# Layer 1's attention: transposes by query tile and two pieces later, values and output products put off, cosine product in place

## The chip, the cores and the metric

The kernel runs on one core of one Trainium2 chip. The metric is the device time of one execution in microseconds (us), the median of several runs.

## The reference, cut to what matters

Four layers act on 4 sequences of 512 tokens of width 256, all in fp32. Each layer normalises its input and adds an attention branch and a feed-forward branch to it. The change touches the attention branch of layer 1 alone, a latent attention with 16 heads:

```
q   = rmsnorm(x @ wq_a) @ wq_b                  # per head: 128 columns without, 64 with rotation
ckv = x @ wkv_a                                 # 64 compressed columns, 64 rotated key columns
k_nope, v = split(rmsnorm(ckv[:64]) @ wkv_b)
q_pe = q_pe * cos + rotate_half(q_pe) * sin     # likewise k_pe
scores = (q_nope . k_nope + q_pe . k_pe) * 192 ** -0.5, causal
out = softmax(scores) @ v, all heads, @ wo
```

Beside it layer 1 has a product-key branch (each token picks 8 of 512 experts, whose rows are gathered from memory) and a gated MLP.

## The kernel before, in words

**Streams and pieces.** Each branch is a Python generator that emits instructions and yields at the end of each piece a number, its planned cost in us. `weave` takes the next piece from the stream that is least far along, relative to its planned total. In layer 1 three streams are woven: `latent_pieces` (the attention), `product_key_pieces` and `glu_pieces`. The program order that comes out is the priority in which a scheduler, with its own estimate of durations, fills each engine's instruction queue; an instruction that it takes to be ready may go ahead of earlier ones on its engine. `tc.keep_in_program_order` ties one instruction behind the one emitted just before it on the same engine. On the chip each engine works through its queue and waits at semaphores.

**Heads and pairs.** The head's key and value weights are folded into the query and the output weights (`carry`, once per group of four heads), so keys and values of all heads are the same latent rows: `kf` (keys, with the rotated part) and `cv` (values, 64 columns). A pair `p` is two heads of one sequence; there are 32 pairs, and `s` from 0 to 63 counts head by head. The loop has four pieces per `s`, `i` from 0 to 3, one for each tile of 128 query tokens.

- `queries(p)` (L707 on): the four query products (L715 to L718), ACT's copy `pes` of the part to be rotated (L721), four transfers on SP's queue that copy `pes` to `psw` with halves of 32 partitions swapped (L723), and the unrotated part into `qf` (L725, L726). It is emitted in piece 1 of the even head before the pair.
- `rotate` (L730 on), three pieces later, on DVE: `pec` = `pes` times cosine (L732), `psw` times sine in place (L733), and two additions into `qf` (L734, L735).
- `probabilities(s, i)`: through `exp_scores` one score product into a bank of the kind "mm" (L577), DVE's mask and minimum into `pr` (L580), ACT's exponential with row sum (L584). After `i` = 3 DVE takes the reciprocal of the sums (L747) and ACT scales the four `pr` tiles (L749).
- `turned(s - 1, j)`: transposes on TensorE of the previous head (L756). For key tile `j` it turns the blocks of query tiles `j` to 3 into one of two banks "tr"; the copy to `PT` (L760) is emitted one piece later, on DVE for even `j` (512 and 256 columns wide), on ACT for odd `j` (384 and 128). `PT` holds 1280 columns, one run for each key tile.
- After the last copy of a pair's second head: the value product, 16 matmuls into a bank "acc" (L800), ACT's copy to `zT` (L806), and after each second pair four output products into banks "acc" (L813), each followed by DVE's addition to `x` in `add_scaled` (L142). The four are emitted one after another, each a piece of its own.

Banks: four "mm", two "tr", two "acc"; the gated MLP's output products (L194) use "acc" as well. The SBUF pool has two buffers for each name unless `bufs` says otherwise.

Of the kernel before, what the change touches and what calls it, by code (L numbers as in the profile page):

```python
# [14 lines left out]
P = 128  # L15
NB, SEQ, DM = 4, 512, 256
# [586 lines left out]
def latent_pieces(c, a, keep, prep, open_pool):  # L603
# [102 lines left out]
    def queries(p):  # L706

        g, b, pair = p // 8, p // 2 % 4, p % 2
        if p % 8 == 0:
            carry(g)  # L710
        wpe0, wpe1, wl0, wl1, _ = weights[g]
        tokens = slice(b * SEQ, (b + 1) * SEQ)
        cols = slice(pair * P, (pair + 1) * P)
        pe, pl = c.ps(), c.ps()
        nc.tensor.matmul(pe, lhsT=wpe0[:, cols], rhs=qa0[:, tokens], start=True, stop=False)  # L715
        nc.tensor.matmul(pl, lhsT=wl0[:, cols], rhs=qa0[:, tokens], start=True, stop=False)
        nc.tensor.matmul(pe, lhsT=wpe1[:, cols], rhs=qa1[:KL, tokens], start=False, stop=True)
# [3 lines left out]
        nc.scalar.copy(pes, pe)  # L721
        for to in range(0, P, 32):
            nc.sync.dma_start(psw[to : to + 32, :], pes[to ^ 32 : (to ^ 32) + 32, :])  # L723
        qf = c.tile(pool, [P, 2, SEQ], "qf")
        nc.scalar.mul(qf[:KL, 0, :], pl[:KL, :], -scale)  # L725
        nc.scalar.mul(qf[KL:, 1, :], pl[KL:, :], -scale)  # L726
        qfs[p] = qf
        return pes, psw, qf

    def rotate(pes, psw, qf):  # L730
        pec = c.tile(pool, [P, SEQ], "pec", bufs=1)
        nc.vector.tensor_mul(pec, pes, cosq)  # L732
        tc.keep_in_program_order(nc.vector.tensor_mul(psw, psw, sinq))  # L733
        nc.vector.tensor_add(qf[:KL, 1, :], pec[:KL, :], psw[:KL, :])  # L734
        nc.vector.tensor_add(qf[KL:, 0, :], pec[KL:, :], psw[KL:, :])  # L735

    def probabilities(s, i):
        p, h = s // 2, s % 2
        b = p // 2 % 4
        if i == 0:  # L740
            totals[s] = c.tile(pool, [P, TPB], "total")
        rinv = totals[s]
        prs[s].append(exp_scores(
            c, pool, late, qfs[p][:, h, :], kf[:, h, b * SEQ : (b + 1) * SEQ], i, rinv[:, i : i + 1]
        ))
        if i == TPB - 1:
            nc.vector.reciprocal(rinv, rinv)  # L747
            for j, pr in enumerate(prs[s]):
                nc.scalar.mul(pr, pr, rinv[:, j : j + 1])  # L749

    def turned(s, j):

        pt = c.ps("tr")
        n = SEQ - j * P
        for i in range(j, TPB):
            nc.tensor.transpose(  # L756
                pt[:, (i - j) * P : (i - j + 1) * P], prs[s][i][:, j * P : (j + 1) * P], c.ident
            )
        copy = nc.scalar.copy if j % 2 else nc.vector.tensor_copy
        return lambda: copy(PTs[s][:, START[j] : START[j] + n], pt[:, :n])  # L760

    START = (0, 512, 896, 1152)
    qfs, prs, totals, PTs, zTs = {}, {}, {}, {}, {}
    rotate(*queries(0))
    copy = None
    yield 4.5
    for s in range(65):
        if s < 64:
            prs[s] = []
        for i in range(TPB):  # L770
# [8 lines left out]
            if i == 0 and s % 2 == 1 and s < 63:  # L779
                rotate(*turning)  # L780
            yield 0.85
            if i == 1 and s % 2 == 0 and s < 62:
                turning = queries(s // 2 + 1)
                yield 2.6
        if copy:
            copy()
            copy = None
        if s > 0:
            del prs[s - 1]
        if s % 2 == 1:  # L790
            continue
        if s == 0:
            continue
# [11 lines left out]
        zTs[pair] = c.tile(pool, [P, SEQ], "zT", bufs=3)  # L805
        nc.scalar.copy(zTs[pair], z)  # L806
        yield 2.1
        if pair == 1:
            wz = weights[g][4]
            for t in range(TPB):  # L810
                po = c.ps("acc")[:, :DM]
                for k in range(2):
                    nc.tensor.matmul(  # L813
                        po, lhsT=zTs[k][:, t * P : (t + 1) * P], rhs=wz[:, k, :],
                        start=(k == 0), stop=(k == 1),
                    )
                add_scaled(c, b * TPB + t, po)
                if g == 3 and t == TPB - 1:
                    c.part_done(b)
                yield 0.85  # L820


def product_key_pieces(c, a, keep, pool, dram, xn):
# [594 lines left out]
```

## Time and profile before

| | |
|---|---|
| median of 3 runs | 3323.99 us (3313.49 to 3325.25) |
| the profiled execution, its own time | 3325.63 us |
| its span | 3323.9 us, granted TensorE clock 0.99 |
| busy in the span: PE, DVE, ACT, POOL | 97%, 57%, 38%, 17% |
| first and last score product of layer 1 | 903.3 and 1572.9 us after the start |
| 900 to 1600 us, busy: PE, DVE, ACT, POOL | 667.97, 502.41, 421.68, 123.86 us |

PE is TensorE's matmuls, PEld its weight loads, DVE VectorE, ACT ScalarE, POOL GpSimd, SP the engine that only issues transfers. Names such as L756 are lines of the kernel before. The ends of matmuls are modelled in the profile, and so a PE that is busy in it is not one at its peak; the starts of matmuls are recorded. A wait is given to the engine and line whose signal came last. Waiting loads of weights cost nothing so long as the matmul before them still runs.

### The profile page before, as it was taken

The page shows a single profiled execution, that of the slowest core. Times are in us where ns is not written, and L with a number is a line of the kernel's source. Part 1 is how long each engine was busy: PE and PEld are TensorE (multiplying, and loading weights), DVE is VectorE, ACT ScalarE, POOL GpSimd, SP SyncE. Part 2 cuts the span into 40 slices and gives each one's busy share as a digit, 9 for nine tenths or more (in the row PEclk, how much of TensorE's full clock was granted, in tenths as well). Part 3 has the DMA queues.
Part 4 walks back from the last instruction along what each step waited for, and adds up shares of the span by engine and source line. Part 5 has one row for each costly group of instructions (what it writes and reads, how often), then busy time and mean ns, then how long its engine had stood idle before and what let it go on. Part 6 is the DMA issues. An engine that isn't in the chain of part 4 may idle for free.

```text
span 3323.9 us, 35406 instructions
## 1 busy us (share of the span) xinstructions
PE 3209.1 (97%) x12524; PEld 1921.4 (58%) x12524; DVE 1894.4 (57%) x4720; ACT 1255.3 (38%) x2870; POOL 579.8 (17%) x445
## 2 busy tenths in 40 slices
PE   8999999998899999999999999999999999999999
PEld 4556555655555555455655555556556665555555
DVE  4777778877788678656655545455455532222222
ACT  4444454443565645568322333333333311111111
POOL 0465556655212133100000000000000000000000
PEclk9999999998999999999999999999999999999999
DMA  3233323323213254301001000000000000000000
GB/s 124 77 105 96 125 85 105 102 96 115 59 43 98 50 146 127 90 14 42 15 1 53 5 1 26 0 20 7 0 20 1 1 19 19 20 21 20 17 0 26
DMA packets 75650, 165.14 MB, mean 50 GB/s; under 512 B 12368, under 2 KB 46288, under 8 KB 70608
## 3 DMA queue, kind: packets, MB, share of 16 engines
q1 hardware_dynamic: 64368, 127.20, 11.9%
q0 software_dynamic: 10240, 33.56, 4.1%
q8 instruction: 98, 1.61, 0.2%
q10 hardware_dynamic: 864, 2.12, 0.2%
q14 instruction: 80, 0.66, 0.1%
HBM read 149.08 MB, written 4.85 MB: 46 GB/s over the span
## 4 chain that ended last, share of the span: by engine, by line
PE 72%; DVE 12%; DMA 6%; issue 4%; POOL 4%; ACT 2%; SPq 0%; DVEq 0%; another core or an unknown queue 0%; POOLq 0%; ACTq 0%
PE mm L125 30%; PE acc L194 10%; PE mm L577 7%; PE mm L133 4%; PE acc L1027 4%; PE acc L593 3%; DMA G<-own 3%; DVE cy L259 2%; PE tr L1023 2%; DVE G L400 2%; DMA e<-in_p_experts,ids 2%; PE tr L756 1%; PE acc L813 1%; PE tr L486 1%; PE acc L800 1%
## 5 line engine op out<-in xcount | busy, mean ns | idle before, releaser
L125 PE MATMUL mm<-xnT,wu 128*128 128x512 f32 x2384 | 1083.4, 597 | 9.2 <-DVE cy L259 4.7
L125 PEld LDWEIGHTS mm<-xnT,wu 128*128 128x128 f32 x2384 | 444.8, 191 | 462.9 <-issue 426.4
L584 ACT ACTIVATE pr<-pr,nm 128x128 f32<-128x128 f32 (+3 forms) x512 | 286.6, 560 | 257.9 <-DVE nm L580 234.0
L186 ACT ACTIVATE sg<-mm 128x512 f32<-128x512 f32 x200 | 119.0, 595 | 697.7 <-PE mm L125 697.5
L187 DVE TENSOR_TENSOR hT<-sg,mm 128x512 f32<-128x512 f32 x200 | 136.9, 684 | 424.3 <-PE mm L125 415.3
L194 PE MATMUL acc<-wu,hT 128*128 128x256 f32 x1600 | 374.1, 382 | 0.0
L194 PEld LDWEIGHTS acc<-wu,hT 128*128 128x128 f32 x1600 | 300.7, 191 | 89.4 <-issue 34.8
L580 DVE CUSTOM_DVE_ANT_0 pr<-mm,late 128x128 f32<-128x128 f32 (+3 forms) x512 | 245.5, 486 | 70.4 <-PE mm L577 55.3
L125 PE MATMUL mm<-xnT,w_in 128*128 128x512 f32 x512 | 231.5, 596 | 6.6 <-DVE cy L259 5.1
L144 DVE SCALAR_TENSOR_TENSOR x<-acc,cw,x 128x256 f32<-128x256 f32 x256 | 123.3, 483 | 182.0 <-PE acc L194 177.1
L917 POOL DMA_INDIRECT e<-in_p_experts,ids x128 | 129.8, 1014 | 359.4 <-DVE x L144 315.1
L400 DVE TENSOR_TENSOR_SCAN G<-G,eye 128x1024 f32<-128x1024 f32 x64 | 155.6, 2431 | 56.4 <-DMA G<-own 56.3
L577 PE MATMUL mm<-kf,qf 128*128 128x128 f32 (+3 forms) x512 | 177.7, 448 | 7.8 <-DVE qf L735 4.4
L1024 DVE COPY PT<-tr 128x128 f32<-128x128 f32 (+3 forms) x256 | 118.7, 481 | 107.1 <-PE tr L1023 107.0
L426 POOL TENSOR_TENSOR G<-G,CB 128x1024 f32<-128x1024 f32 x64 | 151.1, 2361 | 142.2 <-ACT CB L352 81.3
L259 DVE SCALAR_TENSOR_TENSOR cy<-mm,ws,cy 128x509 f32<-128x509 f32 (+2 forms) x216 | 158.4, 741 | 28.9 <-ACT cy L255 25.6
L125 PEld LDWEIGHTS mm<-xnT,w_in 128*128 128x128 f32 x512 | 96.6, 191 | 111.0 <-issue 96.9
L412 ACT ACTIVATE xD<-xc,ws 128x128 f32<-128x128 f32 x256 | 84.3, 391 | 197.7 <-POOL y L449 191.7
L142 DVE TENSOR_TENSOR x<-acc,x 128x256 f32<-128x256 f32 x176 | 73.9, 421 | 148.1 <-PE acc L593 121.1
L577 PE MATMUL mm<-k,q 128*128 128x128 f32 (+3 forms) x512 | 154.9, 446 | 0.8 <-ACT k L1005 0.8
L1027 PE MATMUL acc<-PT,V 128*128 128x512 f32 (+3 forms) x512 | 148.8, 434 | 0.0
L1027 PEld LDWEIGHTS acc<-PT,V 128*128 128x128 f32 x512 | 97.4, 190 | 82.6 <-issue 32.7
(247 smaller groups left out, 4601.3 us busy)
## 6 DMA issues: line engine op xcount, KB each, us to landing
G<-own SPq DMA_DIRECT2D x64, 512.0 KB
w_in<-in_m_units SPq DMA_DIRECT2D x16, 1024.0 KB
eb<-since SPq DMA_DIRECT2D x96, 128.0 KB
wu<-in_o_units SPq DMA_DIRECT2D x8, 1536.0 KB
wo<-in_m_units SPq DMA_DIRECT2D x16, 512.0 KB
psw<-pes SPq DMA_DIRECT2D x128, 64.0 KB
wu<-in_g_units SPq DMA_DIRECT2D x4, 1536.0 KB
wu<-in_f_units SPq DMA_DIRECT2D x4, 1536.0 KB
```

What stands on the lines that cost most here:

```text
L125: c.nc.tensor.matmul(out, lhsT=w[:, d, cols], rhs=c.xnT[:, d, tokens], start=(d == 0), stop=(d == 1))
L133: c.nc.tensor.matmul(out, lhsT=c.xnT[:, d, tokens], rhs=w[:, d, cols], start=(d == 0), stop=(d == 1))
L187: nc.vector.tensor_mul(h, sg, pu)
L194: nc.tensor.matmul(po, lhsT=hT[k][:, t * P : (t + 1) * P], rhs=wd[:, k, :], start=(i == 0), stop=(i == per - 1),)
L259: nc.vector.scalar_tensor_tensor(y[:, j:], src[:, : SEQ - j], conv[:, k, 3 - j : 4 - j], y[:, j:], ALU.mult, ALU.add,)
L400: nc.vector.tensor_tensor_scan(flat, flat, eye.rearrange("p h t -> p (h t)"), 0.0, ALU.mult, ALU.add)
L426: nc.gpsimd.tensor_mul(G, G, seqs[b][2][:, t, :][:, None, :].to_broadcast([P, HG, P]))
L577: nc.tensor.matmul(sc, lhsT=q[:, i * P : n], rhs=k[:, :n], start=True, stop=True)
L580: nc.vector.tensor_tensor_reduce(out=pr, in0=sc, in1=late[:, SEQ - n :], scale=1.0, scalar=-NEG, op0=ALU.add, op1=ALU.min, accum_out=nm,)
L584: nc.scalar.activation(pr, pr, AF.Exp, bias=nm, scale=-1.0, accum_out=total)
L917: nc.gpsimd.indirect_dma_start(out=e, out_offset=None, in_=a["p_experts"], in_offset=bass.IndirectOffsetOnAxis(ap=ids[:, t, k : k + 1], ax ...
L1027: nc.tensor.matmul(z[:, j * P :], lhsT=V[:, j, h, :], rhs=PT[:, j, j * P :], start=(j == 0), stop=(j == TPB - 1),)
```

## The change

- `turned(s, i)` now goes by query tile `i`: it turns the `i` + 1 blocks of one `pr` tile, and one copy spreads them over `PT`, which is laid out so that the blocks of one key tile lie side by side (1664 columns). Copies of query tiles 1 and 3 (256 and 512 columns) are on DVE, of 0 and 2 (128 and 384) on ACT.
- It is emitted two pieces later: for head `s` in pieces 2 and 3 of the next head and 0 and 1 of the one after. The value product follows after piece 1 of the second head after the pair, two pieces later than before.
- The four output products are put in a list, and one is emitted at the end of each following piece.
- `rotate` writes the cosine product over `pes`; `pec` is gone. `wl0` and `wl1` have one buffer each.

```
-        wl0 = c.tile(pool, [P, 256], "wl0")
-        wl1 = c.tile(pool, [P, 256], "wl1")
+        wl0 = c.tile(pool, [P, 256], "wl0", bufs=1)
+        wl1 = c.tile(pool, [P, 256], "wl1", bufs=1)
...
     def rotate(pes, psw, qf):
-        pec = c.tile(pool, [P, SEQ], "pec", bufs=1)
-        nc.vector.tensor_mul(pec, pes, cosq)
+        nc.vector.tensor_mul(pes, pes, cosq)
         tc.keep_in_program_order(nc.vector.tensor_mul(psw, psw, sinq))
-        nc.vector.tensor_add(qf[:KL, 1, :], pec[:KL, :], psw[:KL, :])
-        nc.vector.tensor_add(qf[KL:, 0, :], pec[KL:, :], psw[KL:, :])
+        nc.vector.tensor_add(qf[:KL, 1, :], pes[:KL, :], psw[:KL, :])
+        nc.vector.tensor_add(qf[KL:, 0, :], pes[KL:, :], psw[KL:, :])
...
-    def turned(s, j):
-
+    def turned(s, i):
+
+        if i == 0:
+            PTs[s] = c.tile(pool, [P, LEAD * TPB + P], "PT")
+        PT, pr, n = PTs[s], prs[s][i], (i + 1) * P
+        prs[s][i] = None
         pt = c.ps("tr")
-        n = SEQ - j * P
-        for i in range(j, TPB):
-            nc.tensor.transpose(
-                pt[:, (i - j) * P : (i - j + 1) * P], prs[s][i][:, j * P : (j + 1) * P], c.ident
-            )
-        copy = nc.scalar.copy if j % 2 else nc.vector.tensor_copy
-        return lambda: copy(PTs[s][:, START[j] : START[j] + n], pt[:, :n])
-
-    START = (0, 512, 896, 1152)
+        for j in range(i + 1):
+            cols = slice(j * P, (j + 1) * P)
+            nc.tensor.transpose(pt[:, cols], pr[:, cols], c.ident)
+
+        out = v3(PT, P)[:, i : i + LEAD // P * i + 1 : LEAD // P, :]
+        copy = nc.vector.tensor_copy if i % 2 else nc.scalar.copy
+        return lambda: copy(out, v3(pt[:, :n], P))
+
+    LEAD = SEQ - P
...
+    waiting = []
     yield 4.5
-    for s in range(65):
+    for n in range(65 * TPB + 2):
+        s, i = n // TPB, n % TPB
         if s < 64:
-            prs[s] = []
-        for i in range(TPB):
-            if s < 64:
-                probabilities(s, i)
-            if s > 0:
-                if i == 0:
-                    PTs[s - 1] = c.tile(pool, [P, 1280], "PT")
-                ready, copy = copy, turned(s - 1, i)
-                if ready:
-                    ready()
...
+            if i == 0:
+                prs[s] = []
+            probabilities(s, i)
+        if n >= TPB + 2 and n - TPB - 2 < 64 * TPB:
+            ready, copy = copy, turned(*divmod(n - TPB - 2, TPB))
+            if ready:
+                ready()
+        elif copy:
+            copy()
+            copy = None
+        if i == 0 and s % 2 == 1 and s < 63:
+            rotate(*turning)
+        yield 0.85
+        if i == 1 and s % 2 == 0 and s < 62:
+            turning = queries(s // 2 + 1)
+            yield 2.6
+        if waiting:
+            yield waiting.pop(0)()
+        if not (i == 1 and s % 2 == 1 and s > 1):
+            continue
+
         if copy:
             copy()
             copy = None
...
-                    rhs=PTs[s - 2 + h][:, START[j] : START[j] + SEQ - j * P],
+                    rhs=PTs[2 * p + h][:, j * LEAD + j * P : j * LEAD + SEQ],
...
+        def output(t, g=g, b=b, wz=weights[g][4], zT=dict(zTs)):
+            po = c.ps("acc")[:, :DM]
+            for k in range(2):
+                nc.tensor.matmul(
+                    po, lhsT=zT[k][:, t * P : (t + 1) * P], rhs=wz[:, k, :],
+                    start=(k == 0), stop=(k == 1),
+                )
+            add_scaled(c, b * TPB + t, po)
+            if g == 3 and t == TPB - 1:
+                c.part_done(b)
+            return 0.85
+
         if pair == 1:
-            wz = weights[g][4]
-            for t in range(TPB):
-                po = c.ps("acc")[:, :DM]
...
-                yield 0.85
+            waiting = [lambda t=t, o=output: o(t) for t in range(TPB)]
+    for o in waiting:
+        yield o()
```

More of the change, by code (lines that the diff above doesn't have):

```diff
@@ L765, in latent_pieces @@
     copy = None
+    waiting = []
     yield 4.5
-    for s in range(65):
+    for n in range(65 * TPB + 2):
+        s, i = n // TPB, n % TPB
         if s < 64:
-            prs[s] = []
-        for i in range(TPB):
-            if s < 64:
-                probabilities(s, i)
-            if s > 0:
-                if i == 0:
-                    PTs[s - 1] = c.tile(pool, [P, 1280], "PT")
-                ready, copy = copy, turned(s - 1, i)
-                if ready:
-                    ready()
-            if i == 0 and s % 2 == 1 and s < 63:
-                rotate(*turning)
-            yield 0.85
-            if i == 1 and s % 2 == 0 and s < 62:
-                turning = queries(s // 2 + 1)
-                yield 2.6
+            if i == 0:
[18 more added lines that the diff above has]
+            continue
         if copy:
@@ L787, in latent_pieces @@
             copy = None
[L788 to L793, printed above, removed]
         p = s // 2 - 1
@@ L801, in latent_pieces @@
                     z[h * KL : (h + 1) * KL, j * P :], lhsT=cv[:, b * TPB + j, :],
-                    rhs=PTs[s - 2 + h][:, START[j] : START[j] + SEQ - j * P],
+                    rhs=PTs[2 * p + h][:, j * LEAD + j * P : j * LEAD + SEQ],
                     start=(j == 0), stop=(j == TPB - 1),
                 ))
-        zTs[pair] = c.tile(pool, [P, SEQ], "zT", bufs=3)
-        nc.scalar.copy(zTs[pair], z)
+        zT = zTs[pair] = c.tile(pool, [P, SEQ], "zT", bufs=3)
+        nc.scalar.copy(zT, z)
         yield 2.1
-        if pair == 1:
-            wz = weights[g][4]
-            for t in range(TPB):
-                po = c.ps("acc")[:, :DM]
[L812 to L820, printed above, removed]
+        def output(t, g=g, b=b, wz=weights[g][4], zT=dict(zTs)):
[9 more added lines that the diff above has]
+            return 0.85
+        if pair == 1:
+            waiting = [lambda t=t, o=output: o(t) for t in range(TPB)]
+    for o in waiting:
+        yield o()
 def product_key_pieces(c, a, keep, pool, dram, xn):
```

## The prediction

> **What bounds the kernel now.** I read the page's slices first (TensorE, PE, at nine tenths or more nearly everywhere), then the table of 50 us stretches over layer 1's attention (900 to 1600 us), then the waits of that window, then its timeline. Five stretches; the columns are PE, PEld, DVE, ACT, POOL busy us, granted clock, DMA share, GB/s:
>
> ```profile
> 1100.00:1150.00 50.00, 50.00 (x202) 26.82 (x202) 31.55 (x93) 33.24 (x89) 5.78 (x6) 1.00 0.15 41
> 1150.00:1200.00 50.00, 46.98 (x201) 26.20 (x197) 37.65 (x125) 28.09 (x73) 19.80 (x21) 1.00 0.61 149
> 1200.00:1250.00 50.00, 44.77 (x181) 25.42 (x181) 36.10 (x121) 23.55 (x64) 17.18 (x17) 0.93 0.61 144
> 1300.00:1350.00 50.00, 44.43 (x190) 26.44 (x189) 38.72 (x138) 27.13 (x74) 21.18 (x21) 0.97 0.52 131
> 1450.00:1500.00 50.00, 50.00 (x225) 30.40 (x224) 31.09 (x87) 30.67 (x79) 0.00 (x0) 1.00 0.05 11
> ```
>
> PE is the bound; DVE and ACT have a quarter to a half free. Where the expert gathers run (POOL near 20) PE still loses 3 to 6 us in 50. So only PE's stalls can be won. The waits (engine and line, what it waited for: us in total, times, longest):
>
> ```profile
> PEld tr L756 <- ACT pr L749: 40.3, 83, 1.4
> DVE prod L927 <- DMA e<-in_p_experts,ids: 41.8, 41, 3.8
> DVE pec L732 <- ACT pes L721: 18.5, 9, 5.0
> PEld acc L813 <- DVE x L142: 12.6, 8, 3.1
> PE acc L813 <- DVE x L142: 9.5, 7, 2.7
> PE tr L756 <- ACT pr L749: 4.8, 14, 1.2
> DVE psw L733 <- DMA psw<-pes: 2.9, 4, 0.8
> ```
>
> The first line is weight loads, mostly hidden. To price stalls I took from the timeline the distance between starts of consecutive matmuls, less what the first streams (medians of the trace: 0.429 us for 512 columns, 0.322, 0.216 and 0.108 for 384, 256 and 128; each fp32 product is two such instructions). Over 900 to 1600 us 93 us are left: 41 in some 48 gaps over 0.3 us, 52 in small ones. The large ones: transposes (L756) 15.2 us, of which 10.8 right after a normalising L749 ended; output products (L813) 12.7 us, of which 11.1 until DVE's addition L142 freed an "acc" bank and 1.6 behind the copy of zT; scores (L577) 10.7 us; values (L800) 1.4. The worst of the first kind in the timeline:
>
> ```profile
> 1343.99 0.42 DVE L927 CUSTOM_DVE_ANT_0 prod<-e,tok 128x256 f32<-128x256 f32 x1 [1.38 <-DMA e<-in_p_experts,ids]
> ...
> 1344.34 0.17 DVE L747 RECIPROCAL total<-total 128x4 f32<-128x4 f32 x1
> ...
> 1344.55 1.92 ACT L749 ACTIVATE pr<-pr,total 128x128 f32<-128x128 f32 x4 [2.51 <-DVE dot L927]
> ...
> 1345.00 0.73 PE L756 MATMUL tr<-con,pr 128*128 128x128 f32 x2 [2.82 <-issue]
> ```
>
> DVE stands in order behind a gather, so the reciprocal is late, so ACT's normalising is late, and PE's next transpose stands behind that for 2.8 us.
>
> **What the Trainium skill says.** TensorE: Matmul & The Clock Gate, Architectural detail: TensorE can load weights ahead of running matmuls, while ACT and DVE are strict first-in first-out. The trace agrees: 40.3 us of waiting loads leave 4.8 us of waiting transposes, and the chain above is DVE's order. The same page, What's actually happening: an idle window halves the clock for about 3.4 us. The trace agrees: the granted clock falls to 0.5 five times in the window (near 974, 1202, 1226, 1254, 1346 us), 3.4 us each, each after a stall of 1.4 to 3.0 us. Three of those stalls are of the two kinds that the change moves; the half clock is inside my 93 us. Perfetto Trace Analysis, Tensor Engine Instruction: matmul ends are estimated; indeed 512-column matmuls are listed at 597 ns and start 429 apart, so I use starts. VectorE: DVE Perf Modes, Why PSUM operands drop a tier: fp32 from PSUM runs at the base rate, so the layout of the destination should not matter; the trace agrees: the 512-wide copy takes at most 693 ns at L760 (one block) and 692 at layer 3's L1024 (blocks apart, as the new one).
>
> **The change, part by part.**
>
> 1. Transposes by query tile, two pieces later. Still 10 per head (640 instructions), still copies of 128, 256, 384 and 512 columns, still 128 and 384 on ACT, 256 and 512 on DVE: no work added. A head's first transposes now come 6 pieces after its first score instead of 4, that is two after the piece of the normalising; a piece is 700/260 = 2.7 us, so 5.4 us of lead, and the latest normalising was 3.0 us late. The 10.8 us go; that DVE's lateness may come back elsewhere is rival A. Of the 130 small gaps before transposes (13.2 us) I take half, 6 us (bounds 0 and 13): after two pieces PE waits for one tile per piece, not for four in a row.
> 2. Output products, one per piece instead of four together. 64 of them; each now has about 2.7 us until the next wants a bank, against 0.42 us for the addition L142. Of 12.7 us I take 10, and 2 of the 4.7 us in small gaps there.
> 3. Values put off two pieces. Before, their last input was the 128-wide ACT copy (0.27 us) and 12 of 16 matmuls needed only earlier copies; now all 16 need the copy of query tile 3, 512 wide on DVE (0.69 us), behind DVE's queue. Queued behind a waiting L800: every later PE instruction in the order, scores, GLU products, the next transposes; and ACT's zT for it. The trace shows no such wait for 512 columns; bounds: 0 (other PE work covers it) and 32 x 2.6 = 84 us (2.64 us is the longest PE gap before which a DVE L760 copy had just ended, at 1364 us). Nearest row: the output products, which also wait for DVE on a just released bank, 11.1/64 = 0.17 us each. I take 0.25 us x 32 = 8 us.
> 4. Cosine product in place. pec could start with ACT's copy (0 to 3.5 us after it in the trace) and blocked DVE for 18.5 us; now the product overwrites pes, so it waits for four SP transfers that read pes. They are issued over 2.4 us, and L733, which needs them too, never starts before 3.9 us. Queued behind it on DVE: L733, the additions, then score evictions and gathers' dot products. L733 waits only 2.9 us in all, so its place in DVE's order suits the transfers, and the cosine product takes that place. qf is later by one 0.69 us product; PE starts the first score within 0.1 us of qf in 4 of 32 pairs: 4 x 0.7 = 3, I take 2 (bounds 0 and 10). DVE's 18.5 us are not on the path: 0 (they may help by 5). SP's and POOL's issues are neither more nor moved; POOL's gathers follow DVE's L144 as before.
> 5. Buffers. PT grows by 2 x 384 x 4 = 3072 bytes per partition, pec and second wl0, wl1 free 4096; the single wl pair is rewritten once per eight pairs, after query products long done: 0. The pr buffers are free for two pieces instead of four; L580 waited 2.8 us for transposes, and I add 2 for that (0 to 10).
> 6. Tail: two more pieces at the end of the stream, without new work, beside layer 2's first products: 0 (bounds 0 and 5.4).
>
> Sum: -10.8 - 6 - 10 - 2 + 8 + 2 + 2 = -16.8; the half clocks after two large stalls beyond these are 1.7 us each at most, and I take 2 more: -19 (their slow stretches lie among the small gaps of other lines). Base: the profiled execution took 3325.63 us (span 3323.9 and 1.7 around it), 1.6 above the median 3323.99 of the three runs. 3324 - 19 = **3305 us**.
>
> **Rivals.**
>
> A. *Stalls only move.* DVE is late because of the gathers (41.8 us), and its banks and scores stall PE elsewhere. For it: scores lose 10.7 us already, from 1150 to 1400 us. Against it: DVE has a quarter free even there. Of the 28.8 us gained in items 1 and 2 a third to a half comes back, and the costs of 12 stand: -7 to -2, about 3319.
>
> B. *The values' wait decides; slower.* All 16 matmuls of a pair stand behind DVE's last copy at L800. Without item 3 the sum is -27, so the balance is at 27/32 = 0.84 us per pair, and beyond 44/32 = 1.4 us the kernel is slower by more than 0.5%. At 1.6 us: 51 - 27 = +24, 3348 us. For it: single DVE waits of 2 to 3 us occur. Against it: they are rare, and the scheduler puts other ready PE work ahead of an L800 that it believes not ready.
>
> C. *The change does not do what it says.* Program order is only the priority with which the scheduler fills each engine's queue; it may pull the later transposes forward to the moment at which it believes them ready, as it did with pec. Then 3322 to 3327.
>
> **How the numbers follow.** Forecast 0.42 (3290 to 3312, a little of it above the bound), A 0.27, B 0.18, C 0.10; 0.03 for larger gains (all small gaps at L756 too, and no cost: about 3284). A difference of 0.5%, 16.6 us, is about what a measurement of this kernel can tell from no change. Faster by more (below 3307.4): 0.43. Within: 0.37. Slower by more: 0.20, B and mishaps of A. The range 3284 to 3338 leaves out the worst of B and the best.
>
> **What would show it.** Right: no L813 wait on L142 over 1 us; PE's waits of L756 on L749 near zero; fewer clock dips between 900 and 1500; layer 1 ends some 19 us earlier while layers 0, 2 and 3 keep their lengths. Item 4: the in-place product starts 4 us or more after pes, with a few us of DMA wait. Wrong: L800 waiting on DVE PT for over 27 us, or DVE waiting for the pes transfers by tens of us, or unchanged gaps at L756.

## The result, and the profile after

The changed kernel is slower: 3355.32 us, the median of 4 runs (3349.22 to 3359.12), against 3320.49 for the kernel before on the same chip (4 runs, 3313.49 to 3325.25). The ratio is 1.0100, 95% interval 1.0081 to 1.0119. The forecast was 3305 us and a range up to 3338. The median of the kernel before lay between 3314 and 3324 us on the chips used below, and so every experiment is given as a ratio to the kernel before on its own chip, with its 95% interval. One run of the kernel before without gathers took 12424.64 us, in a slow state, and isn't counted.

The profiled execution took 3351.74 us (span 3349.9), 26.1 us more than that of before; this is the pair that the sums below compare. Layer 1's scores run from 902.9 to 1599.5 us; before, they ended at 1572.9. Layer 3's first score is 26.1 us later as well (1861.9 against 1835.8): the loss lies between the first and the last score of layer 1, and nothing behind it is given back or lost. Three of the forecast's stretches of 50 us, now of the kernel after (PE, PEld, DVE, ACT, POOL busy us, granted clock, DMA share, GB/s):

```profile
1150.00:1200.00 50.00, 50.00 (x213) 30.33 (x212) 27.12 (x82) 29.86 (x80) 2.01 (x2) 1.00 0.18 53
1300.00:1350.00 50.00, 46.64 (x181) 26.91 (x180) 39.86 (x130) 26.76 (x72) 19.37 (x19) 0.93 0.47 120
1450.00:1500.00 50.00, 50.00 (x210) 28.07 (x209) 27.10 (x78) 31.90 (x87) 0.00 (x0) 1.00 0.04 11
```

Read the counts, not the busy time. From 1450 to 1500 us PE is busy all 50 us in both kernels and DMA is quiet, yet the counts are 210 matmul instructions and 225. One stretch may hold longer matmuls than another (from 1400 to 1450 us the counts are 227 after and 219 before, the other way round), so this proves nothing. It raises a question: part of the loss may be no idle time at all, but the same work that keeps PE busy for longer. The waits between 900 and 1626 us (engine and line, what it waited for: us in total, times, longest), which stand against those shown of before:

```profile
DVE prod L934 <- DMA e<-in_p_experts,ids: 51.4, 45, 3.8
PEld tr L759 <- ACT pr L748: 17.7, 15, 2.4
PE tr L759 <- DVE PT L763: 11.6, 9, 2.6
PE mm L577 <- DVE hT L153: 7.2, 3, 3.7
PE tr L759 <- ACT pr L748: 5.6, 5, 1.6
PE mm L577 <- DVE sg L152: 4.1, 3, 1.5
PE tr L759 <- ACT PT L763: 3.7, 6, 1.8
DVE pes L731 <- DMA psw<-pes: 1.7, 1, 1.7
PE acc L803 <- DVE PT L763: 1.3, 3, 0.6
PEld acc L815 <- DVE x L142: 0.5, 2, 0.3
```

What the change aimed at is gone at the output products and in part at the transposes. Output products (now L815) hardly wait for L142 any more (22.1 us of PE and PEld before, 0.5 now). Loads for transposes (L759, once L756) wait 17.7 us for the normalising instead of 40.3, but PE's own waits for it are fewer and longer, 5.6 us in 5 instead of 4.8 us in 14. In its place transposes wait 15.3 us for the copies that empty the "tr" banks (1.0 before), and scores (L577) wait for L152 and L153, DVE's part of the MLP, which empties "mm" banks (11.3 us, 2.0 before).

**Where the time went, as a sum that closes.** The forecast listed gaps. Another view of the same timeline misses nothing: take each matmul's distance from its own start to the next matmul's start, and add these up by what the matmul is, from the first score to the last. Nothing is left out or counted twice, and the sum is the length of the stage. In us:

| start to next start | before | after | difference |
|---|---|---|---|
| scores L577 | 157.1 | 172.5 | +15.4 |
| transposes | 90.8 | 91.1 | +0.3 |
| value products L800 / L803 | 74.1 | 104.2 | **+30.1** |
| output products L813 / L815 | 65.4 | 55.0 | -10.4 |
| query products L715 to L718 | 109.0 | 92.3 | **-16.7** |
| MLP (L125, L194) | 149.1 | 156.2 | +7.1 |
| all else | 24.2 | 25.4 | +1.2 |
| stage | 669.6 | 696.6 | +27.0 |

Each column is one execution. Where only the cosine product is in place (below, no change in time), the rows differ from before by up to 3.6 us, and after a neutral shift of the plan by up to 4.8, so a few us in a row mean nothing.

The two rows in bold are products whose number and sizes the change did not touch, and L803 waits for its copies for only 1.3 us. The timeline shows why; PE alone, start, duration, line, count. A value product of the kernel before:

```profile
1297.05 0.27 PE L756 MATMUL tr<-con,pr 128*128 128x128 f32 x1
1297.25 2.38 PE L800 MATMUL acc<-PT,cv 128*64 128x512 f32 x16
1299.56 0.38 PE L577 MATMUL mm<-kf,qf 128*128 128x128 f32 x1
```

and one of the kernel after:

```profile
1140.06 1.07 PE L803 MATMUL acc<-PT,cv 128*64 128x512 f32 x2
1141.07 1.98 PE L125 MATMUL mm<-xnT,wu 128*128 128x512 f32 x4
1142.98 2.37 PE L803 MATMUL acc<-PT,cv 128*64 128x512 f32 x14
```

The two heads of a pair write to 64 columns each. In order, head 0's and head 1's matmul for a key tile start 0.006 to 0.007 us apart and stream side by side: all 16 instructions take 2.30 us from start to next start (median of 32 products). After, the first two, head 0's first key tile, go off alone (1.0 us), MLP products follow, and then come the other 14, which take as long as all 16 did: head 1's first tile now runs beside head 0's second, 512 columns beside 384, and the heads stay out of step. 3.30 us in the median. Of 32 products other work splits 29 after, 2 before.

Query products show the same the other way round. L717 and L718 use 64 rows each, 0 to 63 and 64 to 127. The kernel before first:

```profile
1101.51 0.32 PE L756 MATMUL tr<-con,pr 128*128 128x128 f32 x1
1101.76 1.12 PE L717 MATMUL mm<-qa,wu 64*128 64x512 f32 x2
1102.82 0.88 PE L756 MATMUL tr<-con,pr 128*128 128x128 f32 x6
1103.62 1.12 PE L718 MATMUL mm<-qa,wl 64*128 64x512 f32 x2
```

and after:

```profile
1113.86 0.69 PE L717 MATMUL mm<-qa,wu 64*128 64x512 f32 x1
1113.87 0.69 PE L718 MATMUL mm<-qa,wl 64*128 64x512 f32 x1
1114.39 0.59 PE L717 MATMUL mm<-qa,wu 64*128 64x512 f32 x1
1114.40 0.59 PE L718 MATMUL mm<-qa,wl 64*128 64x512 f32 x1
```

In the kernel before, transposes between L717 and L718 keep them apart. Other work stands between them in 18 of 32 pairs, after the change in 2, and the eight instructions of the four query products take 3.82 us in the median before and 2.87 after. The Trainium skill says this much (TensorE: Matmul & The Clock Gate, Part 3: Packing small matmuls, The mechanism): matmuls on different tiles of the array run concurrently with starts some 4 ns apart, and matmuls go strictly in order. The traces agree on the starts (6 to 10 ns here). That one stranger between the two costs the whole overlap is what the traces add.

**The granted clock.** The forecast counted five spells of half clock in the kernel before, each after a stall of PE, and expected fewer. They last 3.4 us, as long as it says, though the stalls ahead of them are shorter, 1.4 to 3.0 us. In the stage from the first to the last score they come to 17.1 us before and to 34.1 us, in eight spells, after. The stage as one stretch, before and after (same columns as above):

```profile
903.30:1572.90 669.60, 639.53 (x2687) 362.76 (x2688) 478.81 (x1583) 406.10 (x1071) 121.93 (x120) 0.99 0.29 76
```

```profile
902.90:1599.50 696.60, 651.70 (x2698) 374.39 (x2699) 479.73 (x1587) 407.12 (x1079) 122.11 (x120) 0.98 0.29 73
```

In the profile PE is idle for 44.9 us instead of 30.1, and 17.0 us more at half clock cost another 8.5 us by estimate, if PE would otherwise have streamed. Both are spread over the rows of the sum.

### The profile page after: what moved, and what is told of

The parts are those of the page before. It is cut to its first block, busy times and chain, and to the rows that moved or that the text cites. A ratio compares the mean times of both kernels' runs of the same rounds, so it can differ in the third digit from the quotient of the medians.

```text
span 3349.9 us, 35436 instructions
## 1 busy us (share of the span) xinstructions
PE 3216.9 (96%) x12524; PEld 1927.6 (58%) x12524; DVE 1894.5 (57%) x4720; ACT 1254.0 (37%) x2870; POOL 576.1 (17%) x445
## 4 chain that ended last, share of the span: by engine, by line
PE 70%; DVE 13%; DMA 6%; issue 6%; POOL 3%; ACT 2%; SPq 0%; DVEq 0%; ACTq 0%; POOLq 0%
PE mm L125 30%; PE acc L194 9%; PE mm L577 6%; PE mm L133 4%; PE acc L1034 4%; PE acc L593 3%; DMA G<-own 3%; DMA e<-in_p_experts,ids 2%; PE acc L803 2%; DVE cy L259 2%; PE tr L1030 2%; DVE G L400 2%; PE tr L486 1%; PE tr L759 1%; DVE x L144 1%
## 5 line engine op out<-in xcount | busy, mean ns | idle before, releaser
L125 PE MATMUL mm<-xnT,wu 128*128 128x512 f32 x2384 | 1086.5, 597 | 10.9 <-DVE cy L259 3.6
L125 PEld LDWEIGHTS mm<-xnT,wu 128*128 128x128 f32 x2384 | 443.7, 191 | 468.6 <-issue 429.7
L194 PE MATMUL acc<-wu,hT 128*128 128x256 f32 x1600 | 375.4, 382 | 2.7 <-DVE x L142 2.7
L194 PEld LDWEIGHTS acc<-wu,hT 128*128 128x128 f32 x1600 | 299.9, 190 | 99.5 <-issue 39.1
L125 PE MATMUL mm<-xnT,w_in 128*128 128x512 f32 x512 | 231.5, 596 | 6.9 <-DVE cy L259 5.1
L577 PE MATMUL mm<-kf,qf 128*128 128x128 f32 (+3 forms) x512 | 181.3, 449 | 16.1 <-DVE hT L153 7.2
L142 DVE TENSOR_TENSOR x<-acc,x 128x256 f32<-128x256 f32 x176 | 74.1, 421 | 175.5 <-PE acc L593 121.7
L125 PEld LDWEIGHTS mm<-xnT,w_in 128*128 128x128 f32 x512 | 96.4, 191 | 111.3 <-issue 97.0
L577 PE MATMUL mm<-k,q 128*128 128x128 f32 (+3 forms) x512 | 154.9, 446 | 0.8 <-ACT k L1012 0.8
```

What stands on the lines that cost most here:

```text
L125: c.nc.tensor.matmul(out, lhsT=w[:, d, cols], rhs=c.xnT[:, d, tokens], start=(d == 0), stop=(d == 1))
L194: nc.tensor.matmul(po, lhsT=hT[k][:, t * P : (t + 1) * P], rhs=wd[:, k, :], start=(i == 0), stop=(i == per - 1),)
L577: nc.tensor.matmul(sc, lhsT=q[:, i * P : n], rhs=k[:, :n], start=True, stop=True)
```

## The experiments

There were five groups, each on a chip of its own: the kernels of the first three parts below, four each; the neutral shift with the first three of the four cuts; and the last two kernels. "Late order" means transposes and values two pieces later, as after; "old order" as before.

### One part of the change at a time

**Cosine product in place, alone.**

```
-        pec = c.tile(pool, [P, SEQ], "pec", bufs=1)
-        nc.vector.tensor_mul(pec, pes, cosq)
+        nc.vector.tensor_mul(pes, pes, cosq)
...
-        nc.vector.tensor_add(qf[:KL, 1, :], pec[:KL, :], psw[:KL, :])
+        nc.vector.tensor_add(qf[:KL, 1, :], pes[:KL, :], psw[:KL, :])
```

> The kernel before with one edit: the cosine product overwrites pes, pec is gone. Theory L (the loss comes from putting the transposes and values off by two pieces, so that they become filler whose place in the queue hangs on the two tr banks): no change here, 3320 within 8 us. Theory Q (the loss comes from the query-tile order, where the whole value product stands behind a 512-wide DVE copy): no change, 3320 within 8. Theory C (the in-place product waits for the four transfers and holds DVE's queue): slower by 15 us or more. Theory S (single output products compete with the MLP's for the acc banks): no change.

3328.55 us, 1.0012 (0.9998 to 1.0026): no change that can be told from none.

**Output products one per piece, alone.**

```
+            if waiting:
+                yield waiting.pop(0)()
...
-                yield 0.85
+            waiting = [lambda t=t, o=output: o(t) for t in range(TPB)]
```

> The kernel before with one edit: the four output products of two pairs are emitted one per piece instead of in a row. Theory S: slower by 10 us or more. Theories L, Q and C: faster by 4 to 12 us, since the 12.7 us of gaps before output products go (they went in the changed kernel: 17.4 us of all gaps there became 3.5).

3329.35 us, 1.0010 (0.9998 to 1.0022), neither of the two outcomes expected. Its sum by kinds: output products 65.4 to 54.7 us (-10.7, the size that was priced), transposes 90.8 to 101.3 (+10.5). The saving is there where it was aimed at, and as much is lost at the transposes, where PE now waits 6.5 us for the copies out of the "tr" banks (1.0 before): rival A in its purest form.

**Query tiles at the old places** (with the cosine product in place and one buffer for `wl0`, `wl1`; values where they were).

```
-    def turned(s, j):
+    def turned(s, i):
...
-        copy = nc.scalar.copy if j % 2 else nc.vector.tensor_copy
+        copy = nc.vector.tensor_copy if i % 2 else nc.scalar.copy
```

> The kernel before with the transposes and copies by query tile, at their old places in the program, values and outputs at their old places too. For room in SBUF it also has the in-place product and single wl buffers, so it is read against e1_inplace. Theory Q: slower than e1_inplace by 15 us or more, with the gaps before values grown from 7 to about 20 us. Theory L: within 8 us of e1_inplace.

3344.82 us, 1.0051 (1.0031 to 1.0071): slower with no delay at all. Values cost 104.9 us (+30.8), transposes 84.6 (-6.2). Its timeline holds both a wait and the split:

```profile
1279.26 0.59 PE L800 MATMUL acc<-PT,cv 128*64 128x512 f32 x1
...
1281.59 0.43 DVE L927 CUSTOM_DVE_ANT_0 prod<-e,tok 128x256 f32<-128x256 f32 x1 [0.52 <-DMA e<-in_p_experts,ids]
...
1282.73 0.43 DVE L927 CUSTOM_DVE_ANT_0 prod<-e,tok 128x256 f32<-128x256 f32 x1 [0.71 <-DMA e<-in_p_experts,ids]
...
1283.69 0.68 DVE L760 COPY PT<-tr 128x512 f32<-128x512 f32 x1
...
1284.53 1.98 PE L800 MATMUL acc<-PT,cv 128*64 128x512 f32 x5 [4.05 <-DVE PT L760]
```

The first two matmuls of the product have gone ahead (the second starts at 1279.26 us). DVE waits for two gathers, then copies query tile 3, and PE stands at L800 for that copy: rival B's picture. The next two groups of runs ask whether the wait or the split is the cause.

**Late, but by key tile as before.**

```
-    for s in range(65):
+    for n in range(65 * TPB + 2):
+        s, i = n // TPB, n % TPB
...
-                ready, copy = copy, turned(s - 1, i)
+            at, j = divmod(n - TPB - 2, TPB)
+            ready, copy = copy, turned(at, j)
```

> The kernel before, still by key tile and with output products in a row, but the transposes of a head two pieces later and the value product two pieces later. Theory L: slower by 15 to 35 us, gaps before transposes moving from the normalising (L749) to the copies out of the tr banks. Theory Q: within 8 us of before, or faster by up to 12 because the waits for the normalising go.

3333.09 us, 1.0021 (1.0008 to 1.0035). Query products 91.7 us (-17.3), transposes 83.7 (-7.1), outputs 57.2 (-8.2); values 90.9 (+16.8, 19 of 32 split), scores 170.2 (+13.1), MLP +10.3. So the query products are mended by the delay. With it scores cost more.

### Is it the wait for the last copy?

**The value product one piece later than its last copy.**

```
-        if not (i == 1 and s % 2 == 1 and s > 1):
-            continue
-        if copy:
+        if i == 1 and s % 2 == 1 and s > 1:
             copy()
             copy = None
+        if not (i == 2 and s % 2 == 1 and s > 1):
+            continue
```

> The changed kernel with the value product one piece further from the last copy of its pair: the copy stays after piece 1, the values follow after piece 2. Theory V (the values stand right behind the copy of query tile 3 on DVE, which stands behind dot products that wait for gathers; 22 us of gaps before values after the change, 33 in the query-tile kernel, 7 before): gaps before values fall to about 8 us and the kernel is faster than the changed one by 10 us or more, about 3340. Theory M (DVE's and ACT's lateness stalls PE whatever the order, so the gaps move): the gaps before values fall and others grow, time within 6 us of the changed kernel, about 3355.

`PT` is also taken later here, at its first copy. 3347.53 us, 1.0090 (1.0066 to 1.0114), not told apart from after. 19 products still split, values 98.3 us.

**The last copy on ACT.** ACT and DVE change places, so that query tile 3 doesn't stand behind gathers.

```
-        copy = nc.vector.tensor_copy if i % 2 else nc.scalar.copy
+        copy = nc.scalar.copy if i % 2 else nc.vector.tensor_copy
```

> The changed kernel with the copies of query tiles 0 and 2 on DVE and of 1 and 3 on ACT, so that the 512-wide copy ahead of the values is on ACT. ACT gets 256 and 512 columns in place of 128 and 384. Theory V: faster by 5 to 15 us, about 3345, since ACT does not stand behind gathers. Theory M: within 6 us of the changed kernel, 3355.

3354.38 us, 1.0109 (1.0075 to 1.0143): no help, values 105.4 us, and PE waits 4.7 us at L803 for the copy that is now ACT's. Rival B as it was written, PE standing at L803 for DVE's last copy, is not what makes this kernel slow: in the kernel after itself that wait is 1.3 us.

**Both kernels without gathers.** One constant tile stands for all gathered expert rows; DVE's products on it stay.

```
-        nc.gpsimd.indirect_dma_start(
-            out=e, out_offset=None, in_=a["p_experts"],
...
+        e = same
```

> The kernel before without the expert gathers: all tokens use one constant tile of rows, so that DVE's dot products never wait for a transfer. Left out: the gathers of expert rows. All theories: faster than before, by 20 to 50 us (3275 to 3300), because 42 us of DVE's waits for gathers go. It is the base for the next run.

> The changed kernel with one constant tile of rows in place of the gathers. Left out: the gathers of expert rows. Theory G (the loss is DVE's lateness behind gathers, which the new order meets with less slack): within 8 us of the kernel before without gathers. Theory O (the new order itself costs, by its own waits between PE, DVE and ACT): 20 us or more slower than the kernel before without gathers.

3277.58 us (three runs), 0.9875 (0.9846 to 0.9903), and 3297.88 us, 0.9943 (0.9924 to 0.9961). 20 of the 35 us of loss are there without a single gather. The same 600 us (from 900) of the two, before first:

```profile
900.00:1500.00 600.00, 595.33 (x2569) 342.37 (x2567) 448.36 (x1479) 384.71 (x1015) 0.00 (x0) 1.00 0.10 30
```

```profile
900.00:1500.00 600.00, 589.92 (x2488) 341.47 (x2488) 433.31 (x1443) 369.97 (x984) 0.00 (x0) 0.99 0.10 30
```

Nearly full clock, PE busy for most of both, and 81 instructions fewer done. Their stages (630.3 and 649.2 us) differ by values +29.0, query products -15.7, scores +2.7, and the rest +2.9: without gathers, what is left of the change is almost entirely the two pairings. PE is idle for 5.4 us more of these 600 us, so waits can explain a part of the 18.9 us at most.

### Is it the pairing?

**The second head first.** Head 1's `PT` is complete last. If its matmul leads the pair, nothing of the product can go early, and the 16 stay together.

```
-            for h in range(2):
+            for h in (1, 0):
```

In the kernel after, in the one with query tiles at the old places, and in the kernel after without gathers (as above):

> The changed kernel with one edit: in the value product the second head's matmul is emitted ahead of the first head's for each key tile, so that the chain of 16 begins with the one that needs the last copy and no member goes ahead alone. Theory P (the first head's first matmul is ready early, goes ahead alone, and the heads, which run side by side on the two halves of the array's columns, are out of step from there on: 3.30 us for a value product in place of 2.30, 109.7 us in all in place of 78.8): value products are back at 2.3 us, some 80 us in all, and the kernel takes about 3325, 25 to 33 us less than the changed one. Theory M (lateness of DVE and ACT stalls PE in any order): within 8 us of the changed kernel.

> The query-tile kernel (old places, product in place) with the second head first in the value product. Theory P: value products at 2.3 us, time within 6 us of the in-place kernel, about 3328, which is 17 less than the query-tile kernel. Theory V (each value product stands behind DVE's 512-wide copy): still 3340 or more, since that wait stays.

> The changed kernel without gathers (one constant tile of rows; left out: the gathers of expert rows) and with the second head first. Theory P: 3273 to 3283, the kernel before without gathers took 3278, since the difference of 20 us without gathers is the value products' 105.7 against 75.8 us. Theory O (other waits of the new order): 3290 or more.

No product is split in any of them, and values fall to 75.6, 75.5 and 73.7 us. In time the second and third kernel came out as theory P said, the first as theory M did.

- At the old places 1.0051 becomes 1.0003 (0.9992 to 1.0013), although PE still waits 17.9 us for the last copy at L800: the loss there was the split, not the wait.
- Without gathers 0.9943 becomes 0.9889 (0.9868 to 0.9910), level with before without gathers (0.9875).
- In the kernel after, nothing: 1.0099 (1.0082 to 1.0116). Values give 28.6 us back, and scores go from 172.5 to 190.1, transposes from 91.1 to 103.0. The waits of this last one, at PE:

```profile
PE tr L759 <- DVE PT L763: 14.6, 8, 3.1
PE mm L577 <- DVE qf L734: 8.6, 9, 1.9
PE mm L577 <- DVE hT L153: 8.4, 5, 3.8
PE mm L577 <- DVE sg L152: 5.3, 3, 3.4
```

Such waits of scores for DVE and ACT come to 28.1 us in all (16.0 in the kernel after): PE, freed from 29 us of streaming, waits more for DVE's results and banks. The clock takes another part. PE is at half clock for 54.6 us of the stage instead of 34.1, and the mean granted clock of the four runs is 0.9850, of the kernel after 0.9885: by estimate 0.0035 of 3350 us, some 12 us. Mending one loss uncovered others, and so a single undo in the changed kernel was a poor test.

**The split put into the kernel before.** Head 0's first value matmul is emitted two pieces early. It takes the product's "acc" bank two pieces earlier too, and nothing else changes.

```
+            if i == 2 and s % 2 == 0 and s > 0:
+                z = c.ps("acc")
+                b = (s // 2 - 1) // 2 % 4
+                tc.keep_in_program_order(nc.tensor.matmul(
+                    z[:KL, :], lhsT=cv[:, b * TPB, :], rhs=PTs[s - 2][:, :SEQ],
...
+                if j == 0 and h == 0:
+                    continue
```

> The kernel before with one edit that brings in the suspected cost alone: the first head's first value matmul is emitted two pieces early, after piece 2, and the other fifteen stay where they were; transposes, copies and outputs are untouched. Theory P: value products at 3.0 to 3.3 us where the first is apart, and the kernel 20 to 35 us slower than before, about 3348. Theory M: within 8 us of before.

3328.10 us, 1.0042 (1.0025 to 1.0059), +14 us: more than the 8 us of theory M, less than the 20 to 35 of theory P. Its timeline shows the pattern of the kernel after, made on purpose:

```profile
1302.54 1.07 PE L784 MATMUL acc<-PT,cv 128*64 128x512 f32 x2
1303.55 1.12 PE L577 MATMUL mm<-kf,qf 128*128 128x512 f32 x2
1304.51 0.27 PE L756 MATMUL tr<-con,pr 128*128 128x128 f32 x1
1304.71 2.37 PE L808 MATMUL acc<-PT,cv 128*64 128x512 f32 x14
```

Values +26.6 us, scores -6.6, transposes -3.8, outputs -3.7. PE's waits of output products for L142, which frees "acc" banks, are 5.9 us (9.5 before), so the bank that is held longer doesn't show as a wait. Half of the price comes back at other products. Part of this is the clock: the stage has one spell of half clock (3.4 us) instead of five, and the mean granted clock is 0.9930 in its four runs and 0.9913 in the 15 of before on its chip, by estimate 0.0017 of 3320 us, some 6 us. That a PE which is later finds more of its inputs ready is the likely reason, and isn't shown.

### What is left

**A neutral shift.** One planned cost at the head of the stream, `yield 4.5` to `yield 9.0`, in the kernel before: no work, no dependence and no relative order inside the attention changes, only how the three streams interleave.

> The kernel before with only the plan of the attention stream shifted: its first piece counts 9.0 us instead of 4.5, so the other two streams are woven a little earlier against it. Theory A (any shift of the woven order costs about 0.5 to 1%, the order before being a lucky one): slower by 0.4% or more. All other theories: within 0.25% of before.

3328.49 us, 1.0032 (1.0020 to 1.0045), between the two outcomes expected. This one reweaving did 0.3%; effects of that size below are not findings by themselves.

**Four cuts of the change**: after with second head first and `pec` back (with two `zT` buffers instead of three, for room); after with second head first and the four outputs in a row; old places with second head first and outputs spread; and after with only `pec` back:

```
-            waiting = [lambda t=t, o=output: o(t) for t in range(TPB)]
+            for t in range(TPB):
+                yield output(t)
```

> The changed kernel with the second head first and with pec back (zT in two buffers instead of three, for room). Theory I (the in-place product makes qf late, 20 us of PE waiting for L734): 1.003 of before or less. Theory D (the delay with gathers): 1.008 or more.

> The changed kernel with the second head first and its four output products in a row again: the query-tile kernel with the second head first plus the delay of two pieces. Theory D: 1.007 to 1.011 of before. Theory S (spread outputs): 1.003 or less.

> The query-tile kernel with the second head first (1.0003 of before), transposes and values at their old places, plus outputs one per piece. Theory D: 1.000 to 1.003. Theory S: 1.007 or more.

> The changed kernel with pec back (zT in two buffers, for room) and nothing else: the first head still goes first in the value product, which then takes 3.3 us instead of 2.3. Theory P (the lost pairing costs by itself): 1.007 of before or more, against 1.0031 with the second head first. Theory I (only the in-place product costs in this order): about 1.003.

**And old places, second head first, outputs spread, `pec` kept**, which is the kernel before with the order by query tiles, the second head first and outputs spread, and no delay (`zT` in two buffers here as well):

> The kernel before with query tiles at the old places, the second head first, outputs one per piece, and pec kept (single wl buffers and zT in two, for room). With the product in place it was 0.9979 of before. If the in-place product costs here too, 0.993 to 0.997; if it costs only in the late order, 0.996 to 1.000. A neutral shift of the plan moved the kernel by 0.3%, so less than that is not a finding.

| order | cosine | first head leads | second head leads |
|---|---|---|---|
| late, outputs spread | in place | 1.0100 (after) | 1.0099 |
| late, outputs spread | `pec` | 1.0071 (1.0058 to 1.0084) | 1.0031 (1.0021 to 1.0040) |
| late, outputs in a row | in place | | 1.0056 (1.0039 to 1.0072) |
| old, outputs spread | in place | | 0.9979 (0.9966 to 0.9991) |
| old, outputs spread | `pec` | | 0.9997 (0.9989 to 1.0006) |
| old, outputs in a row | in place | 1.0051 | 1.0003 |

The late kernel with outputs in a row, 1.0056, falls between the two outcomes expected for it. Read as one ladder, the table starts at the query tiles in the old order with `pec` kept, 0.9997; with the delay it is 1.0031, with the first head leading 1.0071, with the cosine product in place 1.0100. Each rung is 0.3 to 0.4%, about the size of a neutral shift, and the intervals of the last two overlap. But the delay costs in all three pairs of kernels by query tile that differ by it (0.34, 0.53 and 1.2%; by key tile it was 0.21%), and head 0 in the lead costs in all pairs but one (0.40, 0.48 and 0.54%, and in the kernel before 0.42%; nothing in the kernel after). Scores and transposes together take 234 to 255 us in every kernel of the old order with gathers, and 254 to 293 in every such kernel of the late order. In the late order with gathers PE waits 9.6 to 17.4 us for the copies out of "tr" banks, in the old one 0.5 to 6.5.

The clock goes the same way. In each of the four pairs that differ by the delay the late kernel's mean granted clock over all its runs is lower (0.9868 against 0.9885, 0.9873 against 0.9902, 0.9850 against 0.9905, and by key tile 0.9876 against 0.9906); times some 3330 us this is 6 to 18 us by estimate, about half of what the delay costs by query tile. The clock is no cause apart from the waits: in the kernels before and after each spell of half clock comes behind a gap of PE.

Why the cosine product in place should cost 0.3 or 0.7% in the late order and nothing in the old one isn't settled. Scores' waits for `qf`, theory I's reason, are no longer with it (8.6 us) than without (9.3). The clock is lower with it (0.9885 against 0.9896, 0.9850 against 0.9868), by estimate 4 and 6 us of the 10 and 23. The kernels with `pec` also have two `zT` buffers instead of three, and no run parts the two edits.

The fastest version, 0.9979, is within a neutral shift of the kernel before. None beats it beyond that.

## Why the prediction was wrong, point by point

Two steps failed. Item 3 priced only the wait at L800, at 8 us, and put the overlap of the two heads' matmuls at nothing, without a reason; values cost 30.1 us, of which 1.3 is that wait. And items 1 and 2 counted stalls as time won, with their return left to rival A; transposes, scores and MLP together cost 22.8 us more instead of less.

- **Item 1 (-16.8 us): much of the named wait went, the time did not.** Loads behind the normalising fell from 40.3 to 17.7 us, but transposes cost 91.1 us after 90.8 of before. By the forecast's own measure, the large gaps before them even grew from 15.2 to 25.8 us. The step that failed is "that DVE's lateness may come back elsewhere is rival A", priced at a third to a half. Transposes now wait for the two "tr" banks (15.3 us, 11.6 of them for DVE's copies), and scores for DVE and "mm" banks (scores +15.4). Fewer clock dips were a sign of being right; there are eight instead of five.
- **Item 2 (-12 us): right at its place**, -10.4 us, -10.7 alone. Alone, as much was lost at the transposes (+10.5).
- **Item 3 (+8 us): wrong in kind, and the largest error.** It asked how long L800 waits and found little, rightly: 1.3 us. Its sentence that all 16 matmuls need the copy of query tile 3 took the pair's two heads for one: head 0's eight need head 0's copy, which is a whole head older than head 1's. So the first of the 16 was ready early. The scheduler put it forward, the side-by-side stream broke, and values cost +30.1 us. `keep_in_program_order` keeps an order, not a neighbourhood. The gap method hid it: it charged each matmul its full streaming time, so lost overlap was no gap.
- **Not in the sum at all: query products, -16.7 us.** By the same mechanism a gain: late transposes no longer fall between L717 and L718. The timeline of before shows other work there in 18 of 32 pairs; the forecast left these products out, because no edit touched them. In every late kernel it is 0 to 3 of 32, in the old order by key tile 15 to 19, in the old order by query tile 3 to 12: the delay mends it, and the order by query tile does in part. That this offset much of item 3's error was luck.
- **Item 4 (+2 us)**: right in the old order (1.0012); in the late order it may be 0.3 to 0.7%, unexplained. DVE waited for the four transfers as little as claimed, 1.7 us.
- **Items 5 and 6**: nothing seen; the layers after layer 1 kept their lengths.
- **Rivals.** A was true, and stronger than priced: alone, it was the whole of item 2. B had the sign and came within 7 us of the time, by luck and for another reason: its place (L800, DVE's last copy) was cleared on ACT without gain and kept in the old order without loss. C was near the mark in its words, a scheduler that pulls forward what it believes ready, but looked for it at the transposes. These did move: the first transposition of a tile starts a median of 7.3 us after its normalising, 0.5 before.

Of +27 us, then: +30.1 from the broken pairing, -16.7 from the mended one, -10.4 from outputs, and +24 (scores, transposes, MLP, the rest) of stalls that moved and of the half clock behind them, by estimate some 8.5 us over all rows. The first three are shown by the sum and by kernels that switch them, as costs at their own products. What they do to the whole time is less sure: the split alone put into the kernel before costs 14 us, and taking it out of the kernel after gains nothing. For the +24 the waits name the banks and DVE. Without gathers the scores cost 2.7 us more, not 15.4, so most of their share comes with the gathers; which of the banks would have to grow is not shown.

## What to carry to other kernels

When two matmuls share the array, what matters is that they are neighbours in the queue; before moving anything, ask for each half when its last input comes, and let the one that comes last lead. Expect only a part of the saving in the end: look at the waits and at the granted clock of the whole stage again. Price an edit by each matmul's distance from start to next start over the whole stage, for all kinds of matmul, the untouched ones too: gaps over a nominal duration show waits and hide lost overlap. And change something neutral once to learn what a mere reweaving does (0.3% here) before taking a third of a per cent for an effect.

## What the runs showed of the hardware that was not expected

- Two heads' fp32 value products on 64 columns each, out of step by one member: 3.30 instead of 2.30 us for the same 16 instructions, without idle time in the profile. Two 64-row products of 512 columns: about 1.05 us side by side, some 2.1 one after the other (L717 and L718 above: 1113.86 to 1114.92, against 1101.76 to 1102.82 and 1103.62 to 1104.67).
- An overlap lost at one product was not all lost in the end: +26.6 us of streaming at values made the kernel before 14 us slower, 28.6 us won back in the kernel after made it no faster, and 26.4 us won back in it without gathers made it some 18 us faster (0.9943 to 0.9889).
- Where the overlap was mended with gathers running, the granted clock was lower: 0.9850 against 0.9885 in the kernel after, 0.9868 against 0.9896 with `pec` (means of all runs, each pair on two chips). Spells of half clock lasted 3.4 or 6.8 us, in the kernels before and after behind single gaps of PE of 1.2 to 3.8 us.
- DVE's waits for gathers are 41.8 us before and 51.4 after; without gathers the kernel before is 1.25% faster (43 us), though DVE is busy 57% of the span. That this is about what DVE waits may be chance.
